# Token attention of a four-layer transformer kernel: query-key blocks of six heads, one spread transfer per head, normalising once per batch

## The chip, the cores and the metric

The kernel runs on one core of a Trainium2 chip. The metric is the device time of one execution in microseconds (us). Engines are named as in the profile: PE multiplies matrices (PEld loads its weights), DVE is the vector engine, ACT the scalar engine, POOL is GpSimd, SP issues most of the DMAs; "SPq" is SP's instruction queue.

## What is computed

The reference runs four transformer blocks on x of 4 batches x 512 tokens x 288 channels, all float32. Each block is a modulated attention and a modulated feed-forward; layer 0's feed-forward is a mixture of four experts (two per token), the others are plain MLPs of width 1152. The attention of layers 0, 1 and 3 is over the tokens of a batch, with 16 heads of 18 channels; that of layer 2 runs over the 16 heads of a token.

```
h = modulate(layernorm(x), shift, scale)
q, k, v = split(h @ w_qkv + b_qkv)              # 16 heads of 18
attn = softmax((q @ k^T) * 18**-0.5)            # 512 x 512 per batch and head
x = x + gate * ((attn @ v) @ w_proj + b_proj)
x = x + gate2 * feed_forward(modulate(layernorm(x), shift2, scale2))
```

## The kernel before, in words

x lies in SBUF for the whole run. `attention` (L529) does layers 0, 1 and 3; `attention_over_heads` (L819) does layer 2, where DVE and POOL form the products elementwise while PE does half MLPs beside it; `experts` does layer 0's feed-forward; one MLP of layer 1 (`early_mlp`) is put into the attention of layer 1.

**Units and steps.** A unit is four heads of a batch: 16 units in a layer. A unit has four steps, one per 128 tokens: 64 steps a layer. Each head's 19 rows (18 channels and one more) lie at the head of a 32-row group of a tile `qk`, queries and keys side by side, so four heads fill 128 partitions. The 19th row is one for the keys, and minus the token's largest score for the queries, so that a product of 19 rows gives a score with its maximum taken off. That is why each unit is scored twice: once LEAD = 6 steps ahead for the maxima (DVE reduces, L668), and once for the weights (ACT's exponential, L661). `set_maxima` (L672) transposes the maxima of four chunks on PE, ACT copies them, and four DMAs put them into the 19th rows.

**A half-step** (`scores`, L648) issues two maxima products and two weights products (L616), then one exponential and two reduces. After the first half's scores `sum_values` (L683) adds four products of weights and values (L690) into the bank SUMS; the values' 19th column is one, so SUMS holds the denominators too. When a unit is done, ACT copies SUMS to an SBUF tile.

**Filler.** Between half-steps `gap` (L139) takes pieces from lists whose entries have a due time and keys that must be marked ready, at most so many us of PE work per gap: PACE is 0.3 after the first half and 1.0 after the second. So the order of work on every engine is fixed at build time. The lists are PE products, lanes (other engines), loads (SP) and spreads (SP). PE's filler in attention, per batch:

- `queries_keys` (L578): five 128-row parts of the 608 query and key rows of all heads, each three products over 96+96+97 rows and 512 columns; ACT copies a part to SBUF.
- `values` (L566): per 128 tokens three products over 96+96+97 rows; DVE copies.
- `spread` (L592): per unit 9 to 10 DMAs that carry the rows of each head's queries and keys (19 rows of 2 KB) to their 32-row group; parts of 128 rows cut some heads in two.
- `set_maxima`; `denominators` (L701): four transposes of a unit's sums, DVE's reciprocal of the 19th columns, POOL's copy of them to 32 columns a head (L710); `normalise` (L714): four transposes back and DVE's multiply; `project` (L724): per 128 tokens four products, one per unit.
- `chunks` (L493): transposes of the normalised input of the next batch.

Products use PSUM banks 6 and 7 in turn (`other`); banks 0–2 take maxima, 3–4 weights. DMAs of a queue are issued in order.

**Start.** SP loads x of four batches, the weights of unit 0's queries and keys (eight DMAs, `load_unit`), the values' weights, three copies of a small constant `selb` (L1730) and the router's weights. POOL scales the queries' weights (L284).

The heart of the gap, for reading the prediction:

```
while True:
    if not started:
        item = take(where, us <= 0)
        if item is None:
            return
        started.append(item)
    if us <= 0 and started[0][0] > flow["now"]:
        return
```

Of the kernel before, what the change touches and what calls it, by code (L numbers as in the profile page):

```python
# [40 lines left out]
UQ = 2 * HG * HO  # L41
NQ = NG * UQ
NQB = -(-NQ // P)
# [15 lines left out]
def tile_dit_blocks(ctx: ExitStack, tc: tile.TileContext, x_in, cond_t, sel_den, sel_b, w_gate, layers, out):  # L59
# [141 lines left out]
    selb = const.tile([P, B, P], F32, name="selb")  # L201
# [9 lines left out]
    mxs = [const.tile([P, TB, HG], F32, name=f"mx{i}") for i in range(2)]  # L211


    spreads_of = [const.tile([P, 2, S], F32, name=f"qk{i}") for i in range(4)]

    def clear():
        for t in spreads_of:
            nc.gpsimd.memset(t, 0.0)
        mark("cleared")
        yield 0.5  # L220
# [7 lines left out]
    def load_attention(l):  # L228

        w, t = layers[l], w_att[l]  # L230

        wqk = wpool.tile([P, NK, NQ + C], F32, tag="wqk", name=f"wqk{l}")
        if l == OVER_HEADS:
            wqk = t["wqkv"] = wqk[:, :, : 3 * C]
            nc.sync.dma_start(wqk[:KP], w["wqkv"].rearrange("(k p) f -> p k f", p=KP))
            nc.sync.dma_start(wqk[KP : KP + 1, NK - 1, :], w["bqkv"])
        else:

            src = w["wqk"].rearrange("(k p) s (h d) -> p k s h d", p=KP, d=HP)
            bias = w["bqk"].rearrange("(o j d) s g -> o s g j d", o=1, d=HP)  # L240
            t["wqk"] = wqk[:, :, :NQ]
            wv = t["wv"] = wqk[:, :, NQ:]

            def load_unit(g, queue):
                for s in range(2):
                    at = slice(g * UQ + s * HG * HO, g * UQ + (s + 1) * HG * HO)
                    for k in range(NK):
                        queue.dma_start(
                            wqk[:KP, k, at].rearrange("p (j d) -> p j d", d=HO),
                            src[:, k, s, g * HG : (g + 1) * HG, :HO],  # L250
                        )
                    queue.dma_start(
                        wqk[KP : KP + 1, NK - 1, at].rearrange("p (j d) -> p j d", d=HO), bias[:, s, g, :, :HO]
                    )
                if g == 0:
                    queue.dma_start(wv[:KP], w["wv"].rearrange("(k p) f -> p k f", p=KP))
                    queue.dma_start(wv[KP : KP + 1, NK - 1, :], w["bv"])
                mark(("loaded", l, g), 6)

            t["load unit"] = load_unit  # L260
            if l > 0:
                for g in range(NG):
                    load_unit(g, nc.sync)
        mark(("loaded", l), 6)
        yield 0.0

    def load_projection(l):
        w, t = layers[l], w_att[l]
        wp = wpool.tile([P, NG, C], F32, tag="wp", name=f"wp{l}")
        t["wp"] = wp  # L270
        if l == OVER_HEADS:
            nc.sync.dma_start(wp[:KP, :NK, :], w["wp"].rearrange("(k p) f -> p k f", p=KP))
            nc.sync.dma_start(wp[KP : KP + 1, NK - 1, :], w["bp"])
        else:
            nc.sync.dma_start(wp, w["wp"].rearrange("(g p) f -> p g f", p=P))
        mark(("projection", l), 6)
        yield 0.0

    def scale_queries(l, g):

        at = slice(g * UQ, g * UQ + HG * HO)
        for k in range(NK):
            q = w_att[l]["wqk"][: KP + (1 if k == NK - 1 else 0), k, at]
            nc.gpsimd.tensor_scalar_mul(q, q, SCALE)  # L284
        mark(("weights", l, g))
        yield 0.2
# [61 lines left out]
    def mod_product(l, half, kinds):  # L348
# [13 lines left out]
        for kind in kinds:  # L362
            at = slice(kind * HP, kind * HP + B)
            nc.vector.tensor_tensor(row[at, :C], pr[at, :C], bada[at, :], ALU.add)
            if kind < 2 and half == 1 and l:
# [8 lines left out]
    def modulation(l, half, kinds=range(3)):  # L374
# [6 lines left out]
        if half == 0:  # L381
# [5 lines left out]
        if half == 0:  # L387
# [18 lines left out]
    def gating(l, half):  # L406
# [4 lines left out]
        for b in range(B):  # L411
            pg = other()
            nc.tensor.matmul(pg[:, :C], selb[at, b, :], row[at, :C], start=True, stop=True)
# [6 lines left out]
    def token_modulation(b):  # L420
# [3 lines left out]
        for kind in range(2):  # L424
            at = slice(kind * HP, kind * HP + B)
            pg = other()
            nc.tensor.matmul(pg[:, :C], selb[at, b, :], row[at, :C], start=True, stop=True)
# [8 lines left out]
    def norm(l, half, b):  # L436
# [46 lines left out]
        elif half == 1:  # L483
# [9 lines left out]
    def chunks(l, half, b):  # L493
# [7 lines left out]
        for k in range(NK):  # L501
            if half == 0:
# [26 lines left out]
    def attention(l, start):  # L529
# [3 lines left out]
        PACE = (0.3, 1.0)  # L533
        qk, sums, done, ex, rec = {}, {}, {}, {}, {}
# [18 lines left out]
        def count(b):  # L553
            counts[b] += 1
            if counts[b] == TB + NQB:
                mark(("first products", l, b))

        def product(to, st, mv, us):

            for k in range(NK):  # L560
                rows = slice(0, KP + (1 if k == NK - 1 else 0))
                nc.tensor.matmul(to, st(rows, k), mv(rows, k), start=k == 0, stop=k == NK - 1)  # L562
                if k < NK - 1:
                    yield us

        def values(b, t):  # L566
            pv = other()[:, :C]
            h = ht[l, 0, b]
            yield from product(
                pv, lambda r, k: h[r, k, t * P : (t + 1) * P], lambda r, k: w["wv"][r, k, :], 0.48  # L570
            )
            nc.vector.tensor_copy(heads(vas[0])[:, t, :, :HD], pv.rearrange("p (h d) -> p h d", d=HD))
            count(b)
            yield 0.48
# [3 lines left out]
        def queries_keys(b, m):  # L578

            h = ht[l, 0, b]  # L580
            n = min(P, NQ - m * P)
            pq = other()
            yield from product(
                pq[:n, :], lambda r, k: w["wqk"][r, k, m * P : m * P + n], lambda r, k: h[r, k, :], 0.86
            )
            t = packed[b, m] = work.tile([P, S], F32, tag="qc", bufs=3, name=f"qc_{l}_{b}_{m}")
            nc.scalar.copy(t[:n, :], pq[:n, :])
            mark(("packed", l, b, m), 1)
            count(b)
            yield 0.86  # L590

        def spread(u):  # L592

            b, g = divmod(u, NG)
            t = qk[u] = spreads_of[u % 4]
            for j in range(HG):
                for s in range(2):

                    at = g * UQ + (s * HG + j) * HO
                    end = at + HO  # L600
                    to = j * HP
                    while at < end:
                        m, r = divmod(at, P)
                        n = min(end - at, P - r)
                        queue = nc.scalar if u == 0 and j >= HG // 2 else nc.sync
                        queue.dma_start(t[to : to + n, s, :], packed[b, m][r : r + n, :])
                        at, to = at + n, to + n
            mark(("spread", l, u), 2)
            if u == N_UNITS - 1:
                mark(("all spread", l), 8)  # L610
# [11 lines left out]
        def only_maxima(step):  # L622
# [7 lines left out]
            for j in range(HG):  # L630
                nc.vector.tensor_reduce(mxs[u % 2][:, c, j : j + 1], pm[j], AX.X, ALU.max)
# [16 lines left out]
        def scores(step, half):  # L648
# [16 lines left out]
            if maxima:  # L665
                for j in range(2):
                    h = 2 * half + j
                    nc.vector.tensor_reduce(mxs[mu % 2][:, mc, h : h + 1], pm[j], AX.X, ALU.max)  # L668
# [3 lines left out]
        def set_maxima(u):  # L672

            pm = other()
            for c in range(TB):
                nc.tensor.transpose(pm[:HG, c * P : (c + 1) * P], mxs[u % 2][:, c], ident)
            t = work.tile([P, S], F32, tag="qc", bufs=3, name=f"maxima_{l}_{u}")
            nc.scalar.copy(t[:HG, :], pm[:HG, :])
            for j in range(HG):
                nc.sync.dma_start(qk[u][j * HP + ONE : j * HP + ONE + 1, 0, :], t[j : j + 1, :])  # L680
            yield 0.5
# [19 lines left out]
        def denominators(u):  # L701
            pd = other()
            for c in range(TB):
                nc.tensor.transpose(pd[:, c * P : (c + 1) * P], done[u][:, c * P : (c + 1) * P], ident)
            r1 = small.tile([P, TB, HG, 1], F32, tag="r1", name=f"r1_{l}_{u}")
            nc.vector.reciprocal(  # L706
                r1, pd.rearrange("p (c j d) -> p c j d", c=TB, j=HG)[:, :, :, ONE : ONE + 1]
            )
            rec[u] = work.tile([P, TB, HG, HP], F32, tag="rows", bufs=1, name=f"rec_{l}_{u}")
            nc.gpsimd.tensor_copy(rec[u], r1.to_broadcast([P, TB, HG, HP]))  # L710
            mark(("reciprocals", l, u), 2)
            yield 0.5

        def normalise(u):  # L714
            pd = other()
            for c in range(TB):
                nc.tensor.transpose(
                    pd[:, c * P : (c + 1) * P], rec[u][:, c].rearrange("p j d -> p (j d)"), ident
                )
            nc.vector.tensor_tensor(done[u], pd, done[u], ALU.mult)  # L720
            mark(("outputs", l, u))
            yield 0.5

        def project(b, t):  # L724
            pp = other()[:, :C]
            for g in range(NG):
                nc.tensor.matmul(  # L727
                    pp, done[b * NG + g][:, t * P : (t + 1) * P], w["wp"][:, g, :], start=g == 0, stop=g == NG - 1
                )
                if g < NG - 1:  # L730
# [6 lines left out]
        def steps(inside=None, tail=None):  # L737
# [3 lines left out]
            for step in range(-LEAD, N_STEPS + 1):  # L741
# [12 lines left out]
                else:  # L754
                    scores(step, 0)
                    sum_values(step - 1)
                    if inside is not None and step in inside:
                        now = flow["now"]
                        close()
                        flow["others"] = (7,)  # L760
                        inside[step]()
                        close()
                        flow["others"] = (6, 7)
# [6 lines left out]
        def ring_of(b, m):  # L770

            m, b = (m - 2, b) if m >= 2 else (m - 2 + NQB, b - 1)
            if b < 0:
                return None
# [1166 lines left out]
```

## Time and profile before

| what | value |
|---|---|
| runs shown, median (lowest to highest), n = 3 | 2476.93 us (2471.87 to 2485.75) |
| the profiled execution's time / its span | 2477.4 / 2475.6 us |
| mean granted clock of PE | 0.941 |
| PE, DVE, ACT, POOL busy, share of the span | 92%, 44%, 34%, 21% |
| layer 0's attention, from the first scores to the experts | 45 to about 445 us |
| experts | about 445 to 916 |
| layer 1's attention, an MLP within it | 916 to 1347 |
| layer 2's attention over heads, half MLPs beside it | 1347 to 1935 |
| layer 3's attention | 1936 to 2300 |
| layer 3's MLP | 2300 to 2475 |

The profile comes from one execution. A group line has the line, engine, operation, tiles and shapes and the count, then the busy time and the mean of one in ns, then the idle time just before and what ended most of it. A windows row has the stretch, its length, the busy time (and instructions) of PE, PEld, DVE, ACT and POOL, the granted clock, the DMA share and GB/s. A timeline row has start, length, engine, line and operation, and in brackets the idle time before and who ended it; on SPq it is the issue of DMAs, not their flight. A waits line has the waiting group, who it waited for, the sum in us, how often, and the longest.

### The profile page before, as it was taken

What the parts mean: (1) busy time and instruction counts of PE and PEld (TensorE: products, weight loads), DVE (VectorE), ACT (ScalarE), POOL (GpSimd) and SP (SyncE); (2) the same over time, 40 slices, a digit from 0 to 9 for tenths busy, and PEclk for the clock granted to TensorE, in tenths of its full rate; (3) what the DMA queues carried; (4) which work ended last, traced back from release to release, by engine and by line L of the source; (5) the groups of instructions that cost most, each with busy time, mean ns of one, the idle gap of its engine ahead of it and who ended that gap; (6) DMA issues with size and microseconds to landing.
All of it is one profiled execution on the core that took longest, in us unless ns stands there. A gap on an engine that the chain in (4) does not pass through costs nothing. (4 is left out here: it accounts for less than half of the span.)

```text
span 2475.6 us, 30149 instructions
## 1 busy us (share of the span) xinstructions
PE 2278.4 (92%) x11188; PEld 1211.7 (49%) x11188; DVE 1087.1 (44%) x1955; ACT 833.6 (34%) x1233; POOL 527.8 (21%) x544
## 2 busy tenths in 40 slices
PE   5999999799998999999998999778599999999998
PEld 2333333367775763333353676455467433333455
DVE  3556656240021124655434768989210445555100
ACT  1344444232222223444335233323223244444311
POOL 2000022130121110110010357778721000001000
PEclk7899999899999998999999999788799799999999
DMA  3211120366644540000000001111210100000000
GB/s 81 97 58 39 51 86 29 96 201 183 188 136 149 181 141 20 12 16 14 26 21 1 22 5 45 21 17 17 24 55 1 28 16 16 14 13 7 1 20 20
DMA packets 163033, 134.23 MB, mean 54 GB/s; under 512 B 81365, under 2 KB 146725, under 8 KB 162886
## 3 DMA queue, kind: packets, MB, share of 16 engines
q1 hardware_dynamic: 159520, 122.39, 17.0%
q0 software_dynamic: 3072, 9.44, 1.2%
q8 instruction: 89, 1.46, 0.2%
q14 instruction: 58, 0.48, 0.1%
q10 hardware_dynamic: 294, 0.47, 0.1%
HBM read 90.67 MB, written 26.25 MB: 47 GB/s over the span
## 5 line engine op out<-in xcount | busy, mean ns | idle before, releaser
L668 DVE TENSOR_REDUCE mx<-banks 128x1 f32<-128x512 f32 x696 | 448.0, 686 | 356.8 <-PE banks L616 356.2
L616 PE MATMUL banks<-qk 32*128 32x512 f32 x3072 | 537.1, 669 | 24.6 <-DMA qk<-qc 13.4
L661 ACT ACTIVATE ex<-banks 128x1024 f32<-128x1024 f32 x348 | 356.4, 1024 | 495.2 <-PE banks L616 493.0
L616 PEld LDWEIGHTS banks<-qk 32*128 32x128 f32 x3072 | 174.5, 191 | 238.4 <-DVE mx L668 97.2
L873 POOL TENSOR_TENSOR pv<-hs,qk 128x1152 f32<-128x1152 f32 x64 | 203.8, 3195 | 50.6 <-DVE ho L885 35.7
L690 PE MATMUL banks<-ex,va 128*32 128x512 f32 x1536 | 210.5, 619 | 0.0
L562 PE MATMUL banks<-ht,wqk 96*128 96x512 f32 (+1 forms) x360 | 189.7, 634 | 1.4 <-POOL wqk L284 0.8
L1472 PE MATMUL banks<-w_b,hid_b 128*128 128x288 f32 x684 | 187.8, 417 | 0.0
L1660 PE MATMUL banks<-ht,w 128*128 128x256 f32 x504 | 135.9, 406 | 36.0 <-ACT hid L1671 35.5
L1452 PE MATMUL banks<-block,w_b 128*128 128x256 f32 x684 | 164.4, 385 | 2.7 <-DMA w_b<-in_w 2.0
L710 POOL COPY rec<-r 128x512 f32<-128x512 f32 x48 | 29.5, 615 | 635.9 <-DVE r L706 562.2
L1682 PE MATMUL banks<-w,hid 128*128 128x288 f32 x504 | 155.6, 446 | 0.0
L1464 ACT ACTIVATE hid_b<-banks,b_b 128x256 f32<-128x256 f32 x171 | 68.7, 473 | 240.3 <-PE banks L1458 167.5
L1472 PEld LDWEIGHTS banks<-w_b,hid_b 128*128 128x128 f32 x684 | 124.0, 190 | 51.5 <-issue 23.1
L1452 PEld LDWEIGHTS banks<-block,w_b 128*128 128x128 f32 x684 | 128.8, 193 | 28.4 <-issue 7.8
L1660 PEld LDWEIGHTS banks<-ht,w 128*128 128x128 f32 x504 | 99.8, 203 | 60.4 <-ACT hid L1671 40.1
L727 PE MATMUL banks<-wp,ot 128*128 128x288 f32 x384 | 117.4, 431 | 5.9 <-DVE upd_a L522 3.5
L1682 PEld LDWEIGHTS banks<-w,hid 128*128 128x128 f32 x504 | 95.7, 202 | 48.0 <-issue 26.6
L523 POOL TENSOR_TENSOR x<-x,upd_a 128x288 f32<-128x288 f32 x48 | 38.0, 791 | 360.5 <-DVE upd_a L522 337.9
L562 PEld LDWEIGHTS banks<-ht,wqk 96*128 96x128 f32 (+1 forms) x360 | 61.2, 191 | 101.7 <-issue 87.8
L727 PEld LDWEIGHTS banks<-wp,ot 128*128 128x128 f32 x384 | 67.6, 192 | 74.9 <-issue 51.2
L690 PEld LDWEIGHTS banks<-ex,va 128*32 128x32 f32 x1536 | 30.9, 109 | 149.4 <-issue 147.7
(224 smaller groups left out, 2577.8 us busy)
## 6 DMA issues: line engine op xcount, KB each, us to landing
w_b<-in_w SPq DMA_DIRECT2D x57, 432.0 KB
w_b<-in_w SPq DMA_DIRECT2D x57, 384.0 KB
qk<-qc SPq DMA_DIRECT2D x327, 38.0 KB
wa<-in_wada SPq DMA_DIRECT2D x7, 864.0 KB
block<-x_mem SPq DMA_DIRECT2D x19, 288.0 KB
y_mem<-y_b SPq DMA_DIRECT2D x19, 288.0 KB
x_mem<-zeros SPq DMA_DIRECT2D x7, 768.0 KB
y_mem<-zeros SPq DMA_DIRECT2D x7, 768.0 KB
```

What stands on the lines that cost most here:

```text
L562: nc.tensor.matmul(to, st(rows, k), mv(rows, k), start=k == 0, stop=k == NK - 1)
L616: nc.tensor.matmul(to, qk[u][r, of, c * P : (c + 1) * P], qk[u][r, 1 - of, :], start=True, stop=True)
L661: nc.scalar.activation(e, WEIGHTS, AF.Exp)
L668: nc.vector.tensor_reduce(mxs[mu % 2][:, mc, h : h + 1], pm[j], AX.X, ALU.max)
L690: nc.tensor.matmul(SUMS[j * HP : (j + 1) * HP, :], vas[0][:, c, at : at + HP], ex[step, j // 2][:, j % 2, :], start=c == 0, stop=c == TB - 1,)
L727: nc.tensor.matmul(pp, done[b * NG + g][:, t * P : (t + 1) * P], w["wp"][:, g, :], start=g == 0, stop=g == NG - 1)
L873: nc.gpsimd.tensor_tensor(prod, sc[i][:, hs, :].unsqueeze(2).to_broadcast([P, GH, HD, NH]), qkv[i][:, 1].rearrange("p h d -> p d h").unsqu ...
L1452: nc.tensor.matmul(banks[:, UP + j, :BT], w1[:, k, j * P : (j + 1) * P], hx[i][:, k, :], start=k == 0, stop=False)
L1464: nc.scalar.activation(t, banks[:, UP + j, :BT], AF.Gelu_apprx_tanh, bias=b1[:, f : f + 1])
L1472: nc.tensor.matmul(banks[:, PY + t, :C], hid[j][:, t * P : (t + 1) * P], w2[:, j, :], start=f == 0, stop=f == NF - 1)
L1660: nc.tensor.matmul(banks[:, UP + j, :BT], full[:, k, (f % 3) * P : (f % 3 + 1) * P], h[:, k, s], start=k == 0, stop=False,)
L1682: nc.tensor.matmul(banks[:, PY + t, :C], hf[:, t * P : (t + 1) * P], w["w2"][f // 3][:, f % 3, :], start=False, stop=f == NF - 1,)
```

## The change

Queries and keys are made in blocks of six, six and four heads, both together: two products over 128 rows each for queries and keys, and two products over the last 32 channels that stand on different 32-row groups of PE (the input's last 32 channels are repeated for that, as the MLPs' input already is). ACT adds the bias and scales the queries. Values are made for two groups of 128 tokens at a time in the same way, DVE adds the bias. A spread is one DMA per head (19 rows of 4 KB), all on SP. One transpose makes the maxima rows of a unit. The sums of a unit are gathered by five DMAs into three tiles by heads (6, 5 and 5 heads of 18 rows; the third holds the 16 denominator rows too). Once per batch four transposes and a reciprocal, four transposes back and an ACT copy make the rows of reciprocals; a DMA writes them to DRAM, each 18 times, three DMAs read them back, and POOL multiplies. The projection has three products instead of four. The filler after first halves is offered no time of its own (PACE), due times are changed, the constant `selb` goes (a column of the identity is broadcast instead), the biases in place of the weights are scaled on POOL, the MLP inside layer 1's attention takes units in twos instead of threes, and the order of the first loads changes. Instructions that differ in number, by engine, in the whole kernel: matmuls 6184 to 5740, ACT 1219 to 1228, DVE 1955 to 1871, POOL 542 to 518, DMAs on SP 1123 to 1225.

```diff
-        PACE = (0.3, 1.0)
+        PACE = (0.0, 1.0)
...
-        def values(b, t):
-            pv = other()[:, :C]
+        def values(b, ts):
             h = ht[l, 0, b]
-            yield from product(
-                pv, lambda r, k: h[r, k, t * P : (t + 1) * P], lambda r, k: w["wv"][r, k, :], 0.48
-            )
-            nc.vector.tensor_copy(heads(vas[0])[:, t, :, :HD], pv.rearrange("p (h d) -> p h d", d=HD))
+            to = [other()[:, :C] for _ in ts]
+            for t, bank in zip(ts, to):
+                for k in range(KF):
+                    nc.tensor.matmul(bank, h[:, k, t * P : (t + 1) * P], w["wv"][:, k, :], start=k == 0, stop=False)
+                    yield 0.48
+            for i, (t, bank) in enumerate(zip(ts, to)):
+                r = slice(i * RC, (i + 1) * RC)
+                nc.tensor.matmul(bank, h[r, KF, t * P : (t + 1) * P], w["wv"][r, KF, :], start=False, stop=True)
...
+            to = [other()[:n, :] for _ in range(2)]
+            for s in range(2):
+                for k in range(KF):
+                    nc.tensor.matmul(to[s], w["full"][:, k, s, at], h[:, k, :], start=k == 0, stop=False)
+                    yield 0.86
+            for s in range(2):
+                r = slice(s * RC, (s + 1) * RC)
+                nc.tensor.matmul(to[s], w["rest"][r, at], h[r, KF, :], start=False, stop=True)
+            t = packed[b, i] = work.tile([P, 2, S], F32, tag="qc", bufs=2, name=f"qc_{l}_{b}_{i}")
+            for s in range(2):
+                nc.scalar.activation(
+                    t[:n, s, :], to[s], AF.Identity, bias=w["bqk"][:n, s, i : i + 1], scale=SCALE if s == 0 else 1.0
+                )
...
             for j in range(HG):
-                for s in range(2):
...
-                        queue = nc.scalar if u == 0 and j >= HG // 2 else nc.sync
-                        queue.dma_start(t[to : to + n, s, :], packed[b, m][r : r + n, :])
+                nc.sync.dma_start(t[j * HP : j * HP + HO], packed[b, i][r : r + HO])
...
         def set_maxima(u):
             pm = other()
-            for c in range(TB):
-                nc.tensor.transpose(pm[:HG, c * P : (c + 1) * P], mxs[u % 2][:, c], ident)
+            nc.tensor.transpose(pm[:n, :P], mxs[u % 2].rearrange("p j c -> p (j c)"), ident)
...
+        def gather_heads(u):
...
+            nc.sync.dma_start(last[at : at + HG, :], done[u][ONE::HP, :])
+            for j in range(HG):
...
+                nc.sync.dma_start(oc[b][k][at : at + HD, :], done[u][j * HP : j * HP + HD, :])
+            mark(("packed heads", l, u), 2)
...
+        def reciprocals(b):
+            pd = other()
+            rows = slice(KP, P)
+            for c in range(TB):
+                nc.tensor.transpose(
+                    pd[:, c * HP : (c + 1) * HP], oc[b][NK - 1][rows, c * P : (c + 1) * P], ident[rows, rows]
+                )
...
+            mark(("reciprocals", l, b), 1)
...
+        def reciprocal_rows(b):
             pd = other()
             for c in range(TB):
+                nc.tensor.transpose(pd[:HP, c * P : (c + 1) * P], rec[b][:, c], ident)
...
+            nc.scalar.copy(t, pd[:HP, :])
+            mark(("reciprocal rows", l, b), 0)
...
+        def normalise(b):
+            rows = dram.tile([NH, HD, S], F32, tag="rec", name=f"rec_rows_{l}_{b}")
+            nc.sync.dma_start(rows, rec[b][1 : 1 + NH, :].unsqueeze(1).to_broadcast([NH, HD, S]))
...
+            for ks in ((0, 1), (2,)):
+                t = work.tile([P, TB, C + 1], F32, tag="rows", bufs=1, name=f"by_{l}_{b}_{ks[0]}")
...
+                    nc.sync.dma_start(room[k], rows[r0:r1, :])
+                for _ in range(3):
+                    yield WAIT
+                for k in ks:
+                    n = (HEADS[k][1] - HEADS[k][0]) * HD
+                    nc.gpsimd.tensor_tensor(oc[b][k][:n, :], oc[b][k][:n, :], room[k], ALU.mult)
+            mark(("outputs", l, b), 2)
...
-                    products, at_step(last if b + 1 == B else last + (7 if l == 0 else 11) + t),
...
+                    products, at_step(last + 5 + t), [("outputs", l, b), ("gate", l, 0), ("projection", l)], project(b, t)
...
-                task(products, at_step(s + TB + 3), [("sums", l, u)], denominators(u))
-                task(products, at_step(s + TB + 5), [("reciprocals", l, u)], normalise(u))
+                task(spreads, at_step(s + TB + 1), [("sums", l, u)] + free, gather_heads(u))
+            task(products, at_step(last + 2), [("packed heads", l, b * NG + NG - 1)], reciprocals(b))
+            task(products, at_step(last + 3), [("reciprocals", l, b)], reciprocal_rows(b))
+            task(spreads, at_step(last + 3), [("reciprocal rows", l, b)], normalise(b))
...
-    for kind in range(3):
-        nc.sync.dma_start(selb[kind * HP : kind * HP + B], sel_b)
...
-        mlp(1, 0, b, TRIOS, home="hm")
+        mlp(1, 0, b, DUOS, home="hm")
```

## The prediction

> **What bounds the kernel now.** I read the page first. Its busy line and the costliest groups give the candidates; the windows by stage then say where each of them counts.
>
> ```profile
> PE 2278.4 (92%) x11188; PEld 1211.7 (49%) x11188; DVE 1087.1 (44%) x1955; ACT 833.6 (34%) x1233; POOL 527.8 (21%) x544
> L616 PE MATMUL banks<-qk 32*128 32x512 f32 x3072 | 537.1, 669 | 24.6 <-DMA qk<-qc 13.4
> L710 POOL COPY rec<-r 128x512 f32<-128x512 f32 x48 | 29.5, 615 | 635.9 <-DVE r L706 562.2
> ```
>
> ```profile
> 1347.00:1935.00 588.00, 506.77 (x2068) 351.73 (x2064) 331.48 (x377) 172.31 (x326) 310.19 (x221) 0.88 0.12 25
> 1936.00:2300.00 364.00, 350.38 (x2000) 130.49 (x2002) 199.77 (x357) 165.19 (x191) 27.16 (x40) 0.96 0.04 12
> ```
>
> The windows row gives length, then PE, PEld, DVE, ACT, POOL, clock, DMA share. 1936–2300 is layer 3's attention: PE is busy 350 of 364 us, DVE 200, ACT 165, DMA 4%. The row above it (layer 2 over heads) is shared by POOL and DVE, and the change leaves that stage's code alone. So I price the change on PE's queue in the attention of layers 0, 1 and 3. The waits of PE in 1936–2300 say how much is lost there today:
>
> ```profile
> PE banks L676 <- DVE mx L668: 5.1, 7, 1.0
> PE banks L704 <- ACT ot L698: 4.2, 5, 1.4
> ```
>
> All waits of that stage sum to 14 us; none is for a DMA. Then the timeline of one step, for prices:
>
> ```profile
> 2086.03 1.07 PE L690 MATMUL banks<-ex,va 128*32 128x512 f32 x8
> 2086.11 1.29 DVE L668 TENSOR_REDUCE mx<-banks 128x1 f32<-128x512 f32 x2 [0.74 <-PE banks L616]
> 2087.02 0.75 PE L727 MATMUL banks<-wp,ot 128*128 128x288 f32 x2
> 2087.70 1.14 PE L616 MATMUL banks<-qk 32*128 32x512 f32 x8
> 2088.77 1.72 PE L727 MATMUL banks<-wp,ot 128*128 128x288 f32 x6
> 2088.94 6.05 SPq L606 DMA_DIRECT2D qk<-qc  x9
> 2090.43 1.14 PE L616 MATMUL banks<-qk 32*128 32x512 f32 x8
> ```
>
> A half-step is a score quartet (1.07 from its start to the next group), in the first half also a sum quartet (about 1.0), then filler: 0.48 a 288-column product, 0.86 a 512-column one (five quartet-to-quartet distances with two or four of them), about 0.53 for four transposes. Without filler two halves take 4.63 (1.29 and 3.34 at 2015.74), since the next weights need the exponential's bank and the next maxima the reduces; so filler up to 1.5 us a step is free.
>
> **The change, part by part.**
>
> *Filler on PE, per batch.* Before: queries and keys 15x0.86 = 12.9; values 12x0.48 = 5.8; maxima, denominators and reciprocals 4x3x0.53 = 6.4; projection 16x0.48 = 7.7; sum 32.7. After: queries and keys 12 full and 3 paired slots, 12.9; values 8+2 slots, 4.8; one transpose per unit, 4x0.25 = 1.0; two groups per batch, 0.4+0.53; projection 12x0.48 = 5.8; sum 25.4. The saving, 7.3x12 batches = 88 us, is an upper end: some falls in halves that were already at the floor. I summed both orders of PE's queue half by half with the prices above (and 0.24 for a second half whose first half had none): before 369, 271+63 and 341 us in layers 0, 1, 3; after 358, 262+61 and 331. Difference **-32**. The unpriced remainder (341 against 364 measured in layer 3) is waits and small gaps.
>
> *The pairs.* That two 32-row products share a slot rests on L616: eight matmuls of 32 rows take 1.14, where a full 512-column one takes 0.86 alone. If pairs do not overlap: 3x0.86+2x0.48 = 3.5 per batch, 42 us; I take 0.
>
> *Old waits that go.* The denominators' transposes waiting for ACT (4.2, 5.1, 3.1 us in layers 3, 1, 0) and the maxima's for the last reduce (6.4, 6.3, 4.7): 30 us, **-30**. What is late next: the single maxima transpose still waits for that reduce. Where it heads a half with products behind it, they wait too: about 5 times a layer, 0.5 each, **+7**.
>
> *Banks.* A query-key block and a value pair each take both product banks, and their reads (two ACT passes of about 0.78, or two DVE adds of about 0.45) come at the end. The next filler waits: 0 to 8 us a layer; I take 4.7, **+14**.
>
> *Early MLP.* Groups of two units make five remainder slots in place of three: **+2**.
>
> *Start-up.* Now the first scores stand waiting, and the clock falls:
>
> ```profile
> 31.47 5.71 SPq L1730 DMA_DIRECT2D selb<-in_sel_b  x3
> 45.22 2.04 PE L616 MATMUL banks<-qk 32*128 32x512 f32 x2 [12.39 <-DMA qk<-qc]
> ```
>
> ```profile
> 36.00:46.00 10.00, 0.78 (x1) 0.49 (x2) 1.28 (x6) 0.00 (x0) 1.04 (x1) 0.50 0.09 24
> 46.00:70.00 24.00, 22.94 (x48) 7.30 (x46) 7.91 (x13) 0.59 (x1) 0.00 (x0) 0.50 0.20 64
> ```
>
> The change deletes the selb loads (5.7) and puts two query-key blocks and the values ahead of the first scores, so PE works while the spread flies. Some 47 DMAs at 0.55 put SP's first spread at about 28, heads 0 and 1 at about 36 instead of 45. If the clock holds at 1 through 36–70 another 10 or so is saved. Bounds 0 and -22; I take **-14**. The Trainium skill's page "TensorE: Matmul & The Clock Gate", Part 1, says that an idle window of some 3.4 us halves the clock; the rows agree here (0.50 after the 12.39 wait), and by it alone a PE fed before 36 would keep all of it.
>
> *Normalising once a batch.* In place of 16 transposes, POOL's copy (0.61) and DVE's multiply (0.69) per unit there is a chain: ACT copies the sums, five gather DMAs per unit on SP, four transposes and a reciprocal, four more transposes, an ACT copy, a 590-KB write, two reads, two POOL multiplies, a read, a multiply, then projection. No row has this chain; its links do: ACT 0.58 (L698), SP 0.6 per DMA, a landing of 1.3–3, rows from scratch (576 KB):
>
> ```profile
> 1794.08 4.29 DMA rows<-scratch
> ```
>
> POOL 1.4 for 128x576 (L523-like rows at 2466.72, 128x1152 at 3.2). First transposes: in the written order they come 3 half-steps (some 9.6) after the sums; copy (behind the exponential, about 2) + five issues (3) + landing (2.5) + queueing is 7.5 to 14. So 0 to 4.5 per batch; I take 0.9 for nine batches, **+8**. Projection: some 7 halves (18.7) after the second transposes, against 1.2+4.3+3.5+2.8+0.6+3+1.3 = 16.7, up to 21: 0 to 4; **+8** for nine. At the three layers' ends only 2 or 3 us of other products separate sums and first transposes: 2 to 8 each, against 1–1.5 now; net **+10**.
>
> *SP.* Spreads become four DMAs of 19 rows, 76 KB, in place of nine. Their bytes are equal, and in the trace's packet records such a DMA sends its 2048-byte packets one after another, 84 ns each (19 rows 1.6 us), while 108- to 128-row ones run wide. So a unit's spread still lasts about 12.5 us, hidden today (PE waited 14.4 for DMAs, all at start-up). Blocks are ready 5 halves (13 us) or more before their first score; a unit's last two heads could be 0 to 2 late, about 6 times a layer: 0 to 36; I take 0, as the row of waits shows none.
>
> The Trainium skill's "DMA: Bandwidth & Descriptors", "Why a DMA increments its semaphore by 16 and not by 1", gives the rule that speaks against the change: the slowest dimension chooses the engines, 19 rows get one, always the lowest, and 18, 4 or 288 rows include that one. By it gathers and the 590-KB write wait behind spread packets, up to 12 us each, and an estimate by the page would be the last rival's sum.
>
> *Loads.* Ahead of layer 3's attention 34 weight DMAs run on SP from 1771.0 to 1794.1, then the read for which PE stands 18.7 us:
>
> ```profile
> 1774.91 3.15 DMA wqk<-in_wqk
> 1778.12 3.15 DMA wqk<-in_wv
> ```
>
> After, 32 DMAs stand there, 16 of them biases of 38 single numbers: -4 to +10 by 0.5 to 1 us each; I take **0**. The projection's weights become 17 DMAs for one, 10 us of SP, behind the first spreads and long before projection; POOL's 36 multiplies (about 1.4 each, 50 us) replace 48 copies (29.5) where it idles (27 of 364 us busy): 0 each, and if that cover fails it is in the projection's 0 to 4. ACT gains 6x0.78 for 5x0.59 per batch (1.7) and loses about 0.3 per unit: 0.
>
> Sum: -32-30+7+14+2-14+8+8+10+0 = **-27**. From the profiled execution, 2477.4 (span 2475.6; the median of the runs shown, 2476.9, is the same within 0.5): 2450.
>
> **Rivals.**
>
> *The new chain is hidden.* No bank waits, none for reciprocals or projection, ends as now, start-up at its bound: -32-30+7+2-22 = -75, **2402**. For it: DMA is 4% busy in layer 3 and the halves between are some 17 us. Against it: the ends of layers have no cover.
>
> *Gain lost in equal part.* The price points above each at mid-bound: reciprocals 2.2x9 = 20 and projection 2x9 = 18 (in place of 16), banks 8x3 = 24 (in place of 14): +32 with -27, about 0: **2480**. Pairs that do not overlap give the same (+42 on work, about 15 of it above the floor by the 32/88 ratio: 2465).
>
> *Slower: SP's queue.* The third read waits at its head until POOL has made two multiplies, 1.2+4.3+4.3+2.8 = 12.6 us after the second transposes, and the next unit's maxima rows are issued behind it in most batches; their scores follow about 3 halves (8) after their transpose. If spread packets hold up the write by a half of their 12.5 as well, the maxima land 6 late and gathers 3 late: 9x(6+3) = 81 for the 16 I took, -27+65 = +38: **2515**. It decides from the point at which write and reads take over 12 together. For it: PE's queue is in order, and today SP already waits for spreads before maxima (12.7 us in 17 times). Against it: the transpose comes 4 halves (10.5) after the chain's start in batches where it is behind.
>
> **Chances.** 0.42 forecast (2432–2465), 0.18 hidden, 0.16 lost, 0.24 SP's queue. 0.5% (12.4 us) is about what a measurement tells here: faster 0.60, same 0.16, slower 0.24. The range takes most of both outer cases: 2395 to 2515.
>
> **What would show it.** PE's wait for gathered sums at the reciprocals' transposes near 1 us a batch; projection's first wait on POOL under 2; weights' scores waiting for maxima rows near 0; no more wait of denominators on ACT; first scores near 36–38 with the clock near 1; layer 3's stage some 10 us shorter. Wrong if maxima rows or gathers cost PE over 5 us a batch, or if layers 0, 1 and 3 keep their lengths though PE has less work.

## The result, and the profile after

The changed kernel takes 2596.4 us (median of 4 runs, 2580.2 to 2601.4) where the kernel before takes 2481.3 (4 runs): a ratio of 1.045, 95% interval 1.039 to 1.052. It is slower by about 4.5%; 2450 was forecast, and the upper end of the range was 2515. The profiled execution has a span of 2595.6 us, 120.0 more than the one before.

From the page of the changed kernel, the busy line and the scores' group; L632 is what L616 was:

```profile
PE 2294.1 (88%) x10732; PEld 1207.9 (47%) x10732; DVE 1052.6 (41%) x1871; ACT 832.3 (32%) x1257; POOL 542.2 (21%) x520
L632 PE MATMUL banks<-qk 32*128 32x512 f32 x3072 | 640.0, 697 | 26.3 <-DMA qk<-tops 17.0
```

PE has fewer instructions (10732 where 11188 stood), yet is busy 15.7 us longer. The scores, untouched in number and form, went from 537.1 to 640.0 us. So it isn't PE's work that grew: PE waits more, and works at half speed more often. The windows of layer 0's steady part show it, kernel before first, then after (length, PE, PEld, DVE, ACT, POOL, granted clock, DMA share, GB/s):

```profile
200.00:300.00 100.00, 98.26 (x591) 37.25 (x588) 61.40 (x132) 46.21 (x56) 6.52 (x9) 1.00 0.11 41
300.00:400.00 100.00, 98.12 (x566) 38.11 (x558) 62.44 (x147) 43.80 (x53) 15.82 (x25) 1.00 0.17 61
```

```profile
200.00:300.00 100.00, 89.33 (x478) 33.34 (x475) 48.53 (x86) 40.59 (x50) 8.58 (x9) 0.90 0.18 56
300.00:400.00 100.00, 89.90 (x471) 32.09 (x469) 56.69 (x133) 38.14 (x49) 17.41 (x25) 0.91 0.23 70
```

PE was never throttled there before; now its clock is 0.90 on average and it is busy 90% instead of 98%. Over the whole trace the time granted at half clock rose from 294.9 to 465.6 us. The longest waits of PE over the whole span say what it stood for, two rows of the kernel before first, then the changed kernel's seven largest:

```profile
PE banks L1425 <- DMA block<-x_mem: 20.6, 3, 9.0
PE banks L616 <- DMA qk<-maxima: 1.0, 2, 0.5
```

```profile
PE banks L1714 <- ACT hid L1725: 38.7, 9, 11.8
PE banks L1478 <- DMA block<-x_mem: 35.9, 3, 14.0
PE banks L744 <- DMA oc<-ot: 29.0, 10, 5.1
PE banks L692 <- DVE mx L684: 25.7, 22, 1.9
PE banks L968 <- DMA rows<-scratch: 22.9, 2, 22.6
PE banks L692 <- ACT qc L608: 18.1, 5, 14.8
PE banks L632 <- DMA qk<-tops: 17.0, 7, 5.4
```

The first and the fifth stood before too (35.5 and 18.7, in an MLP and in layer 2). Of the five others, three are for DMAs: experts' token blocks (20.6 before), the gathered sums at the reciprocals' transposes (new) and the maxima rows (1.0 before); the wait for ACT's copies of query-key blocks goes back to one, as ACT waits there for a spread to have read their buffer (14.8 of the 18.1 come once, at the start).

The time can be split: while PE is busy at half clock, half of that time is lost to the clock. The last column, what PE's work would take at full clock, is an estimate by that, in us:

| | span | PE idle | PE busy | of it at half clock | work at full clock |
|---|---|---|---|---|---|
| before | 2475.6 | 197.2 | 2278.4 | 215.4 | 2170.7 |
| after | 2595.6 | 301.5 | 2294.1 | 339.1 | 2124.6 |

So PE has 46 us less work, stands idle 104 us longer, and loses 62 us more to the clock: together the 120.

By stages, in us (first exponential as a time; layer 0 from there to its last scores; then up to each next attention's scores; the last column over the whole trace):

| | first exp | layer 0 | experts | layer 1 | MLP inside | rest of 1 | layer 2 | layer 3 | end | half clock |
|---|---|---|---|---|---|---|---|---|---|---|
| before | 89.6 | 357.3 | 469.1 | 301.4 | 54.5 | 77.0 | 586.9 | 365.7 | 174.0 | 294.9 |
| after | 108.2 | 387.8 | 501.2 | 312.0 | 51.8 | 74.9 | 599.6 | 388.9 | 171.3 | 465.6 |

The loss is at the start (18.6), in layer 0 (30.5), in the experts (32.1), in layer 3 (23.2), and some in layers 1 and 2.

One instance in layer 3, from the changed kernel's timeline (SP's and PE's rows):

```profile
2142.97 2.55 SPq L623 DMA_DIRECT2D qk<-qc  x4
2146.98 0.54 SPq L732 DMA_DIRECT2D oc<-ot  x1
2147.57 3.00 SPq L736 DMA_DIRECT2D oc<-ot  x4
2158.47 0.40 PE L744 MATMUL banks<-ident,oc 32*128 32x32 f32 x4 [3.79 <-DMA oc<-ot]
```

A spread's four DMAs are issued at 2143, the gathers of a unit at 2147. In the packet records the spread's 76 packets of 4096 bytes go out one after another, most of them 159 ns long, from 2144.2 to 2157.7. Of the gathers' 76 packets of 2048 bytes 67 are through by 2151.6; the last nine go only from 2157.7 to 2158.5, when the spread's are through. PE's transposes begin at 2158.47. And further on in the same layer:

```profile
2179.51 0.64 SPq L765 DMA_DIRECT2D rec_rows<-rec  x1
2189.04 5.75 SPq L774 DMA_DIRECT2D by<-rec_rows  x3
2191.97 2.48 POOL L779 TENSOR_TENSOR oc<-oc,by 108x512 f32<-108x512 f32 x2 [140.49 <-DMA by<-rec_rows]
2194.89 2.69 SPq L696 DMA_DIRECT2D qk<-tops  x4
2198.09 2.64 PE L632 MATMUL banks<-qk 32*128 32x512 f32 x4 [4.80 <-DMA qk<-tops]
```

The write of reciprocal rows takes 9.5 us until the first read can be issued; the third read waits at SP's head for POOL's two multiplies; the maxima rows come behind it, and PE stands 4.8 us.

The experts' loss has spreads in it as well, those of layer 1's first units, which SP issues among the experts' loads:

```profile
786.56 21.43 SPq L623 DMA_DIRECT2D qk<-qc  x8
825.57 5.46 PE L1505 MATMUL banks<-block,w_b 128*128 128x256 f32 x12 [6.96 <-DMA w_b<-in_w]
848.10 1.09 PE L1478 MATMUL banks<-ident,block 128*128 128x128 f32 x4 [14.02 <-DMA block<-x_mem]
```

When several spreads come one after another, SP's own issue is held: these eight DMAs of two units take SP 21.4 us, and the experts' weights and token blocks come behind them in its queue.

### The profile page after: what moved, and what is told of

Same layout as the page of the kernel before. It is cut to its first block, busy times and chain, and to the rows that moved or that the text cites. A ratio compares the mean times of both kernels' runs of the same rounds, so it can differ in the third digit from the quotient of the medians.

```text
span 2595.6 us, 29217 instructions
## 1 busy us (share of the span) xinstructions
PE 2294.1 (88%) x10732; PEld 1207.9 (47%) x10732; DVE 1052.6 (41%) x1871; ACT 832.3 (32%) x1257; POOL 542.2 (21%) x520
## 5 line engine op out<-in xcount | busy, mean ns | idle before, releaser
L632 PE MATMUL banks<-qk 32*128 32x512 f32 x3072 | 640.0, 697 | 26.3 <-DMA qk<-tops 17.0
L632 PEld LDWEIGHTS banks<-qk 32*128 32x128 f32 x3072 | 234.7, 200 | 339.9 <-DVE mx L684 128.6
L709 PE MATMUL banks<-ex,va 128*32 128x512 f32 x1536 | 226.0, 659 | 0.0
L779 POOL TENSOR_TENSOR oc<-oc,by 90x512 f32<-90x512 f32 (+1 forms) x36 | 45.0, 1264 | 865.5 <-DMA by<-rec_rows 778.1
L1505 PE MATMUL banks<-block,w_b 128*128 128x256 f32 x684 | 170.3, 394 | 8.4 <-DMA w_b<-in_w 7.0
L601 PE MATMUL banks<-ht,wqk 128*114 128x512 f32 (+1 forms) x288 | 148.0, 629 | 7.9 <-DVE r L748 4.0
L1736 PE MATMUL banks<-w,hid 128*128 128x288 f32 x504 | 150.2, 433 | 0.0
L910 DVE TENSOR_TENSOR pq<-banks,qk 128x1152 f32<-128x1152 f32 x64 | 86.1, 1345 | 44.8 <-issue 21.8
L456 DVE BATCH_NORM_STATS2 st<-x 128x6 f32<-128x288 f32 x128 | 56.1, 439 | 107.5 <-POOL x L1749 91.0
L1562 POOL DMA_INDIRECT outs<-y_mem,places x32 | 30.7, 961 | 301.3 <-DMA w_b<-in_w 178.2
L1677 PE MATMUL banks<-w,hid 128*128 128x288 f32 x360 | 92.1, 410 | 0.0
```

The lines of the kernel that those rows point to most:

```text
L601: nc.tensor.matmul(to[s], w["full"][:, k, s, at], h[:, k, :], start=k == 0, stop=False)
L632: nc.tensor.matmul(to, qk[u][r, of, c * P : (c + 1) * P], qk[u][r, 1 - of, :], start=True, stop=True)
L709: nc.tensor.matmul(SUMS[j * HP : (j + 1) * HP, :], vas[0][:, c, at : at + HP], ex[step, j // 2][:, j % 2, :], start=c == 0, stop=c == TB - 1,)
L910: nc.vector.tensor_tensor(prod, QUERIES[i % 2][:, :C].rearrange("p (h d) -> p h d", d=HD)[:, hs, :].unsqueeze(2).to_broadcast([P, GH, NH, ...
L1505: nc.tensor.matmul(banks[:, UP + j, :BT], w1[:, k, j * P : (j + 1) * P], hx[i][:, k, :], start=k == 0, stop=False)
L1677: nc.tensor.matmul(banks[:, t, :C], hf[:, t * P : (t + 1) * P], w["w2"][f // 3][:, f % 3, :], start=False, stop=f == NF - 1,)
```

## Experiments

Two theories at the outset. **A, one engine**: a DMA of 19 rows goes out packet by packet on one DMA engine; each of the change's other DMAs has a share on that engine and stands behind it. (The packet records show the order and times of packets, not the engine.) **B, the chain**: SP's order and the round trip through DRAM are slow in themselves. Times are medians beside the kernel before on the same chip.

**Spreads of 16 and 3 rows, in the changed kernel** (e1_wide):

```diff
-                nc.sync.dma_start(t[j * HP : j * HP + HO], packed[b, i][r : r + HO])
+                for d0, d1 in ((0, 16), (16, HO)):
+                    nc.sync.dma_start(t[j * HP + d0 : j * HP + d1], packed[b, i][r + d0 : r + d1])
```

> The changed kernel, with each head's spread of 19 rows split into two DMAs, of 16 rows and of 3 rows; nothing else. Theory A (one engine): a 19-row DMA sends its 4096-byte packets one after another, 159 ns each, 12 us per unit, and the gathers, the write of reciprocal rows and the start-up's copies stand behind them; each wait of 3 to 5 us on PE is followed by some 7 to 10 us at half clock. Then PE's waits at the reciprocals' transposes fall from 29 to under 8 us, those for maxima rows from 17 to under 5, ACT's wait for spreads at the start from 51 to under 15, the time at half clock from 466 to under 380, and the kernel takes 2490 to 2530. Theory B (SP's queue and the round trip of normalising are long in themselves): waits stay within a third, 2570 to 2610, since SP issues 192 DMAs more.

Measured 2488.9 where before takes 2484.9: ratio 1.001 (0.999 to 1.003). That one edit takes away the whole loss, some 107 us. The waits in this kernel:

```profile
PE banks L745 <- DMA oc<-ot: 2.2, 2, 1.5
```

```profile
PE banks L633 <- DMA qk<-tops: 13.3, 7, 3.3
```

The first fell from 29.0; the second only from 17.0, less of a fall than A expected (under 5). ACT's waits for spreads fell from 64.3 to 27.2 us, all at the start, where A expected under 15; half clock fell from 465.6 to 347.2. The 76 packets of a unit of layer 3 now go out in 5.2 us (2183.9 to 2189.2) in place of 13.5, several at a time. Nor is SP held as long: two units' spreads among the experts' loads take 10.6 us for 16 DMAs in place of 21.4 for 8, and the experts' stage 474.9 in place of 501.2.

```profile
743.99 10.58 SPq L624 DMA_DIRECT2D qk<-qc  x16
```

**The control: as many DMAs, split the other way** (e6_split_one), queries and keys apart, 19 rows each:

```diff
-                nc.sync.dma_start(t[j * HP : j * HP + HO], packed[b, i][r : r + HO])
+                for s in range(2):
+                    nc.sync.dma_start(t[j * HP : j * HP + HO, s, :], packed[b, i][r : r + HO, s, :])
```

> The changed kernel, each head's spread split into two DMAs again, but by queries and keys: 19 rows of 2 KB each. As many DMAs for SP as with 16 and 3 rows, the same bytes. Theory A (one engine carries a 19-row DMA): nothing is gained, 2585 to 2620. Rival (two smaller DMAs per head land earlier whatever their rows): 2490 to 2530, as with 16 and 3 rows.

Measured 2601.1, ratio 1.044 (1.041 to 1.048): nothing gained. Number and order of DMAs and the bytes of a head equal those of the run above; the rows of a DMA differ, and with them its bytes (38 and 38 KB in place of 64 and 12) and the size of a packet. The 2048-byte packets again go out one after another, 84 ns each. Its waits:

```profile
PE banks L745 <- DMA oc<-ot: 22.1, 9, 5.4
```

With this and e1_wide it is shown that the row count of the spread is what costs: neither more nor smaller DMAs help, 16 and 3 rows do.

**The same split in the kernel before** (e3_before_wide; `queue.dma_start` for rows 0–16 and 16–19 wherever a piece has more than 16 rows):

> The kernel before, with each 19-row spread split into 16 and 3 rows. Theory A: its spreads are hidden in the steady part (PE waited for a spread only at the start, 13 us), so 2465 to 2485, the gain only at the start. Theory B: SP issues some 330 DMAs more, 2480 to 2500.

Measured 2482.7, ratio 0.9985 (0.997 to 1.000), which lies in both ranges: no change worth the name. Its spreads are as serial, but little that PE needs stood behind them: it waited 1.0 us for maxima rows in all, and the first exponential came no earlier (89.4).

**The old normalising per unit in the changed kernel** (e4_old_norm): `denominators`, `normalise`, the four-product `project` with their due times and the single weight DMA are put back. To make room in SBUF three small statistics tiles have fewer buffers.

```diff
-                task(spreads, at_step(s + TB + 1), [("sums", l, u)] + free, gather_heads(u))
-            task(products, at_step(last + 2), [("packed heads", l, b * NG + NG - 1)], reciprocals(b))
...
+                task(products, at_step(s + TB + 3), [("sums", l, u)], denominators(u))
+                task(products, at_step(s + TB + 5), [("reciprocals", l, u)], normalise(u))
```

> The changed kernel with the old denominators, normalising and projection per unit (no gathers, no reciprocal rows through DRAM, projection weights in one DMA); blocks of six heads, one spread DMA per head and single maxima transpose stay. Theory A: the serial spreads still hold up the start and the copies of blocks, the old transposes come back as some 15 us of time: 2545 to 2570. Theory B: what was slow is the normalising chain, so it goes back to 2480 to 2515.

Measured 2600.3, ratio 1.046 (1.044 to 1.048). Both expectations missed, B by most: without the chain nothing is won. The waits show why:

```profile
PE banks L628 <- DMA qk<-tops: 31.7, 13, 6.1
```

Now PE stands for the maxima rows 13 times. In four units of the 48 the packet records show the last of their packets 2 to 9 us after SP issued them, while a spread's packets go out, and PE then waits 1.9 to 6.1 us. In the changed kernel their packets are through 1.3 to 1.6 us after the last issue in every unit; there they are late at SP's head. So the serial spread holds up this kernel too; which DMA behind it is waited for depends on what else is there.

**The same, with spreads of 16 and 3 rows** (e7_wide_old_norm; both edits):

> Spreads of 16 and 3 rows, and the old denominators, normalising and projection per unit in place of the chain through DRAM: what is left of the change are the blocks of six heads, paired remainders, one maxima transpose. Theory C (with wide spreads the chain still costs waits for maxima rows behind the third read, 13 us and the clock after them, and gives PE less filler): 2470 to 2500, level with the version with the chain (2489). Rival (the chain's saving in PE work shows): 2500 to 2525, slower by the 30 us of transposes and products that return.

Measured 2511.9, ratio 1.011 (1.005 to 1.017): 88 us faster than with 19 rows, 23 slower than e1_wide. So the rival holds: the normalising once a batch is worth something as soon as its DMAs aren't held up, some 20 us with an interval from about 8 to 40 (four runs, 2500 to 2530; the fewer buffers are in it). In the profiled executions PE's work at full clock, by the estimate above, is 62 us less with the chain (2127.2 in e1_wide, 2188.8 here), while idle time (231.6 and 213.6) and the clock (263.7 and 202.2 us busy at half clock) give most of that back. The forecast's idea that it saves time was right; its cover was missing.

**Maxima rows on ACT's queue, in the changed kernel** (e5_tops_act):

```diff
-                nc.sync.dma_start(
+                nc.scalar.dma_start(
                     qk[u][j * HP + ONE : j * HP + ONE + 1, 0, :].rearrange("o (c q) -> o c q", c=TB),
```

> The changed kernel with the maxima rows' four DMAs per unit issued on ACT's queue in place of SP's; nothing else. Theory A: the rows no longer stand behind the third read in SP's queue, but still behind spread packets: PE's wait for them falls from 17 to about 8 us, ACT pays 2.4 us a unit: 2575 to 2605. Theory B: SP's queue is the cause: 2530 to 2565.

Measured 2670.9, ratio 1.075 (1.073 to 1.078), far worse than either. ACT's waits in it:

```profile
ACT ex L677 <- DMA qk<-tops: 103.8, 26, 8.9
```

ACT issues in order too. The transfers were no quicker (3.2 to 7.3 us from a unit's first issue to its last packet, 3.3 to 7.9 on SP), and the exponentials now stood behind them, 26 times.

**Wide spreads for the first four units of layer 0 alone** (e12_wide_start; the edit of e1_wide under `if l == 0 and u < 4`):

> The changed kernel with 16 and 3 rows for the first four spreads of layer 0 alone. Theory A: the start's wait of ACT for spreads (51 us) and PE's 15 us behind it go, nothing else: 2570 to 2582, some 20 less than the changed kernel. Rival (the lost time is the steady part's alone, the start being under other waits): 2590 to 2602.

Measured 2573.4, ratio 1.038 (1.035 to 1.042): 17 to 23 us of the 107 (by the ratios, by the medians) are the start. The first exponential came at 85.2 instead of 108.2; all other stages stayed within some 4 us of the changed kernel's.

**The chain's DMAs on POOL's queue, with wide spreads** (e8_wide_pool):

```diff
-            nc.sync.dma_start(rows, rec[b][1 : 1 + NH, :].unsqueeze(1).to_broadcast([NH, HD, S]))
+            nc.gpsimd.dma_start(rows, rec[b][1 : 1 + NH, :].unsqueeze(1).to_broadcast([NH, HD, S]))
...
-                    nc.sync.dma_start(room[k], rows[r0:r1, :])
+                    nc.gpsimd.dma_start(room[k], rows[r0:r1, :])
```

> Spreads of 16 and 3 rows, and the write of reciprocal rows and its three reads issued on POOL's queue in place of SP's. If SP's head (the third read waiting for POOL's multiplies) is what still delays maxima rows: PE's wait for them falls from 13 to under 4 us, 2465 to 2482. If not, 2485 to 2495, POOL's slower issue taking what is won.

Measured 2475.3, ratio 0.996 (0.994 to 0.9985) to the kernel before: 12 us below e1_wide by the ratios, 13.7 by the medians. PE's wait for maxima rows fell from 13.3 to 5.6 us. In e1_wide SP issues the maxima rows of five units 3.8 to 5.3 us after ACT's copy, right behind one of the chain's reads; here none of the five waits so. So B is true as a smaller, second cause: the chain at SP's head. Which of them it is isn't shown, as the write and the three reads moved together. This is the fastest version found, ahead of the kernel before by 0.4%.

**PACE back at 0.3, with wide spreads** (e9_wide_pace: `PACE = (0.3, 1.0)`):

> Spreads of 16 and 3 rows, and PACE back at 0.3 after first halves. In the version with wide spreads the first halves without filler last 2.6 us on average where 2.07 of PE work stands in them. Theory D (idle first halves cost what the filler saved): 2440 to 2470, the maxima transposes wait less for the last reduce (31 to under 15 us). Rival (halves are at their floor whatever their filler): 2480 to 2500.

Measured 2484.7, ratio 0.999 (0.997 to 1.0015). The waits for the last reduce went only from 31.2 to 29.5 us; theory D falls. Against e1_wide the gain is within the intervals.

**Both** (e13_pool_pace):

> Spreads of 16 and 3 rows, the chain's DMAs on POOL's queue, and PACE at 0.3 as before the change. Each of the two last gained alone (14 and 4 us against wide spreads alone). If they add: 2465 to 2472 where the kernel before takes 2481 to 2486. If filler in first halves only moves the chain's DMAs against other work: 2474 to 2485.

Measured 2484.4 where before takes 2489.7 on this chip, ratio 0.997 (0.995 to 0.9995): no gain over e8_wide_pool (0.996) is seen. Had they added, some 0.994 would be expected, just outside the interval.

**A later maxima transpose**, on top of e8_wide_pool, with PACE 0 (e10_late_t) and 0.3 (e11_late_t_pace):

```diff
                 if half == 1 and mc == TB - 1:
-                    mark(("maxima", l, mu))
+                    mark(("maxima", l, mu), 2)
```

In e10_late_t the first weights' scores of six units of 48 are ordered ahead of their own unit's maxima transpose, so that kernel leaves out a wait that the result needs.

> The version with spreads of 16 and 3 rows and the chain's DMAs on POOL's queue, and the maxima of a unit marked ready one gap later, so that their transpose less often heads a second half right behind the last reduce. There PE waited 32 us for that reduce in 28 places. If those waits cost what they show: 2445 to 2465, the waits down by some 15 us. If the later maxima rows are then missed by the scores: 2475 to 2500.

> The same with PACE back at 0.3, so that most transposes (28 of 48) follow the sums of a first half and filler stands in both halves. If first halves without filler and transposes right behind the reduce are what keeps the filler's saving from showing: 2435 to 2460, waits for the last reduce below 12 us. If not: 2470 to 2490.

Measured 2587.1 (ratio 1.043, 1.040 to 1.047) and 2521.4 (1.018, 1.014 to 1.021), both above every range given. The wait for the last reduce indeed vanished, but the maxima rows were late instead; in e10_late_t, then in e11_late_t_pace:

```profile
PE banks L633 <- DMA qk<-tops: 81.7, 24, 20.6
```

```profile
PE banks L633 <- DMA qk<-tops: 35.3, 16, 6.7
```

So the transpose can't come a gap later: its rows are due within microseconds.

## Why the prediction was wrong, step by step

- **SP, the spreads: the step that failed.** The text priced the serial spread at 0 because its own scores came late enough, "hidden today". That was right for the spread itself (PE waits 0.9 us for one) and for the kernel before (e3_before_wide, no change). What it left out of the sum is what stands behind the spread: the gathers, the buffers of blocks, and, as SP's issue is held, the experts' loads and its own later DMAs. By e1_wide against the changed kernel that is some 107 us, the whole loss, and by the control it is the rows that cost it. How much of it is packets behind packets and how much SP's held issue wasn't separated. The write of reciprocal rows is a small part: SP waits for it 92.2 us in twelve batches, and 82.1 in e1_wide. The rule of the Trainium skill's "DMA: Bandwidth & Descriptors", "Why a DMA increments its semaphore by 16 and not by 1", that 19 rows get one engine, cited against the change, agrees with the pair of runs at 16 and 3 against 19 rows (2489 and 2601 us).
- **The last rival had this mechanism, and was too small**: +65 over the forecast against some 146. It left out the clock. Half-clock time rose by 171 us; PE was busy in 124 us of that, which costs some 62 beside the waits themselves. In the steady parts a wait of 3 to 5 us is mostly followed by 7 to 10 us at 0.50. It also left out the start and the experts.
- **First transposes**: 8 forecast, 29.0 measured (10 waits); 2.2 once spreads are wide. The four links were put at 7.5 to 14 us from the sums on; from ACT's copy to the transposes, the nine inside a layer took 10.5 to 12.3, and PE waited for eight of them. So the range was right and the 0.9 taken per batch too small: the queueing.
- **Projection's wait**: 8 forecast, 5.8 measured. The chain from ACT's copy (2189.2) to the first product (2206.7) took 17.5 us in e1_wide against the 16.7 summed, although its write took 7.5 until the first read and not 4.3.
- **Start-up**: -14 forecast, +18.6 measured. The first scores came at 47.4, not at 36 to 38 (45.2 before; 47.3 in e1_wide too): PE comes to them straight from products that the new order puts ahead. SP's first spread was issued at 34.5, not 28, and the copy of a third block waited until the spread had read one of only two buffers:

```profile
94.37 1.27 ACT L608 ACTIVATE qc<-banks,bqk 114x512 f32<-114x512 f32 x2 [19.57 <-DMA qk<-qc]
```

  That spread stood in SP's queue behind the 17 projection weights (57.3 to 77.1), which I had called hidden. Their issue was itself held, by the spreads ahead of them: in e1_wide it takes 6.3 us and not 19.8. With wide spreads the start gains 4 (89.6 to 85.9).
- **Old waits**: of the 30 to go, the denominators' 14.5 went; the maxima's did not, but grew from 16.7 to 28.7, where I had -17+7. That the missing filler in first halves makes the transpose head second halves, right behind the reduce, doesn't explain it: with the filler back (e9_wide_pace) the wait is 29.5. Why it grew stays open.
- **Filler on PE**: the sign holds. By the estimate above PE has 46 us less work (42 in e8_wide_pool), where the lists gave 88 as an upper end and the sum took 32. What that work would have saved is not shown in one run: in e8_wide_pool PE is idle 27 us longer than before and loses 4 more to the clock.
- **Pairs**: they overlap, as forecast. Two 32-row products side by side take 1.08 us, where the sum had one slot of 0.86 and two slots would be 1.72:

```profile
52.32 1.08 PE L605 MATMUL banks<-ht,wqk 32*76 32x512 f32 x4
```

- **Not priced at all**: the experts (+32.1). Right behind layer 0's last scores the changed kernel and e1_wide are alike (PE busy 36.2 and 38.6 of 64 us). The difference comes later, at 818 to 848, behind the spreads of layer 1: 7.0 us for weights and 14.0 for a token block (2.0 and 9.0 before, none over 1.1 in e1_wide). With wide spreads the stage is +5.8.

What stays open: even with wide spreads and the chain off SP's queue the kernel is only 0.4% faster than before, not the 27 us forecast. The waits for the last reduce (32.3 us) are the largest that remain in the attention; both attempts at them cost more elsewhere, so that no run shows what they are worth.

## What to carry to other kernels

Ask of a transfer not only whether it lands in time, but what is queued behind it, among its packets and in the issuing engine's queue; a row count like 19 makes a slow transfer that is harmless until something urgent stands behind it. Putting many small transfers into few large ones can change their row count, and so how their packets go out: look at that first. And price a wait of PE at more than its length where the trace shows the clock halving after such waits: here 104 us of idle time came with 62 us lost to the clock.

## What the runs showed of the hardware

- A DMA of 19 rows between SBUF tiles sends 4096-byte packets one at a time, mostly 159 ns each (2048 bytes: 84). The same rows as 16 and 3 take 5.2 us per unit instead of 13.5, though SP issues twice as many DMAs.
- Some packets of a later DMA wait behind such packets even if all its others are through: nine of 76 gather packets came 6 us after the rest.
- Such DMAs also hold the engine that issues them when many follow one another: eight, for two units, took SP 21.4 us; two units' 16 DMAs of 16 and 3 rows took 10.6.
- Single waits of 1.7 to 2.0 us were followed by 3.4 to 7 us at half clock (in e8_wide_pool a wait of 1.93 from 2276.5 and 0.50 from 2279.9 to 2283.3; in the changed kernel 1.70 at 477.0 and 2.03 at 411.3), but not always (2.09 at 458.1). The Trainium skill's "TensorE: Matmul & The Clock Gate", Part 1, gives about 3.4 us of idleness for it; here shorter ones were followed by it in places.
- DMAs issued on ACT's queue held up ACT's exponentials for 103.8 us in 26 waits.
